# Adding the causal mask on VectorE, inside the search for the maximum, in the one-head banks of a differential-attention layer

## The chip, the cores and the metric

The kernel runs on one core of one Trainium2 chip. The metric is the device time of one execution in microseconds, as the median of three runs. One more execution was taken by the hardware profiler; every duration and share below is from that one.

## What is computed

Two layers run one after the other on an input of 4 sequences of 1024 tokens with 128 features. Each layer is x + s * silu(g), with s an attention and g a mixture of experts, both of the layer-normalized x.

Layer 0 is an attention of 16 heads with relative positions, without a causal mask. Layer 1 is a causal differential attention, and the change is there:

```python
q = (x @ Wq.T).reshape(B, S, 2 * H, hd).transpose(0, 2, 1, 3) * scaling   # 2H = 16 heads, hd = 8
k = (x @ Wk.T).reshape(B, S, 2 * H, hd).transpose(0, 2, 1, 3)
...
scores = jnp.einsum('bhqd,bhkd->bhqk', q, k)
causal = jnp.triu(jnp.full((S, S), -jnp.inf, dtype=scores.dtype), 1)
attn = jax.nn.softmax(scores + causal, axis=-1)
attn = attn.reshape(B, H, 2, S, S)
w = attn[:, :, 0] - lam * attn[:, :, 1]
```

A softmax needs the largest score of each row. The kernel finds it ahead of the exponentials, in what it calls a search.

## The kernel before

**Tiling.** Tokens go in tiles of 128, so a sequence has 8 tiles. Heads go in groups of 4 (HG). A step is one layer, one sequence, one group of heads and one pair t of query tiles, with m = 0 or 1 in the pair, so that the query tile is i = 2t + m. There are 64 steps in each layer. A step of layer 1 runs through key blocks 0 to 2t + 1, and each of them is one slot of the written-out order. In a slot TensorE forms the transposed scores of four heads (st, line 911), ScalarE takes their exponential (eT, line 949), and TensorE multiplies it with the values one slot later (o, line 958). The row maximum, negated and cut in three bfloat16 parts (lines 869, 884, 886), has been written as extra rows into the queries by then, so that the product of line 911 comes out with the maximum already taken off.

**Searches.** Some slots ahead of a step, TensorE forms the same scores untransposed into a PSUM bank of 512 columns (s, line 792, in score), and VectorE takes the maximum of each row (mx, line 852, in causal1). For a query tile i there are n = i + 1 key blocks, cut into a first part of up to 4 blocks and a second part of the rest. A part of one block puts four heads in one bank, a part of two blocks puts two, and parts of three or four blocks put one head in a bank. The part that ends at the diagonal has to be masked. TensorE does that by a product of the identity with a triangle of 0 and -3e38 (mask_q, bfloat16), which it accumulates onto the last 128 columns of each head (masked, line 831). The transposed scores are masked in the same manner with mask_k, also on line 831; there the bank is named st.

**The order.** Nothing is left to a scheduler. A list of slots is gone through one by one; every piece of work has been given its slot in advance, and within a slot the order in which the code calls is the order of each engine. Searches go two to a slot (RATE), and end 7 slots ahead of their step (LEAD). The expert products of layer 1 (lines 634 and 654), the next sequence's preparation and the routing (lines 534 to 566, VectorE) are spread over the slots. Engines meet by semaphores alone. The banks s, bank, turned_m and turned all come from one pool of three PSUM banks (ps_s), so TensorE can fill a bank only after VectorE has read what was in it three allocations earlier. At the end of a step VectorE copies the sums out of PSUM (os, line 969), and TensorE turns them (turned, line 977).

**A form that exists already.** Layer 0's near0 adds the position bias and takes the maximum in one call of tensor_tensor_reduce (line 808). In the trace that call is two instructions of VectorE: CUSTOM_DVE_ANT_0, which adds, writes the sum and keeps the maximum, and DVE_READ_ACCUMULATOR2_ANT, which writes the maximum out. Searches of that form alternate with plain ones there (far0, line 827).

**Pools.** The pool two has two buffers for each tag. The tag rows holds layer 0's position rows (line 722 fills them on ScalarE, line 731 completes them on GpSimd, a DMA stores them), and is not used in layer 1.

Of the kernel before, what the change touches and what calls it, by code (L numbers as in the profile page):

```python
# [9 lines left out]
F32 = mybir.dt.float32  # L10
# [3 lines left out]
ALU = mybir.AluOpType  # L14
AX = mybir.AxisListType

P = 128
NB = 4
# [4 lines left out]
HG = 4  # L23
NG = NH // HG
NQ = 4
# [4 lines left out]
FMAX = 3.4028234663852886e38  # L30

FLOOR = -3.4028232635611926e38
MASK = -3.0e38
GW = 512
BW = 3 * P
# [28 lines left out]
def both_layers(ctx, tc, a, out, x1d, g1d, flag):  # L64
    nc = tc.nc
    const = ctx.enter_context(tc.tile_pool(name="const", bufs=1))
    one = ctx.enter_context(tc.tile_pool(name="one", bufs=1))
    two = ctx.enter_context(tc.tile_pool(name="two", bufs=2))
# [62 lines left out]
    for pre in ("L0_attn_", "L1_attn_"):  # L131
# [28 lines left out]
        pattern=[[1, NE]],  # L160
        base=-NE,
        channel_multiplier=0,
# [126 lines left out]
    for m in range(2):  # L289
        pair = []  # L290
        for side in "lr":
            t = const.tile([NR, HG, S], BF16, tag=f"ks{side}{m}", name=f"ks{side}{m}")
# [4 lines left out]
    for m in range(2):  # L297
        t = const.tile([P, HG, GW], F32, tag=f"pos{m}", name=f"pos{m}")
# [3 lines left out]
    for m in range(3):  # L302
        t = dconst.tile([P, HG, GW], F32, tag=f"skew{m}", name=f"skew{m}")
# [7 lines left out]
    def after(n, f):  # L311

        if clock[0] is None or n == 0:
            f()
        else:
            todo.setdefault(clock[0] + n, []).append(f)
# [364 lines left out]
    def load_keys(q, g):  # L681
        q.ks[g] = turn("ks", stacks)
        n = 0
        for t, d in zip(q.ks[g], q.kd):
            view = d.rearrange("(h r) t -> r h t", r=3 * HD)[:, g * HG : (g + 1) * HG, :]
            for s in range(3):
                after(n, lambda t=t, s=s, v=view: nc.sync.dma_start(t[24 * s : 24 * s + 24], v))
                n += 1

    def load_queries(st):  # L690
        q, g, t = st.q, st.g, st.t
        st.qs = six.tile([NR, HG, 2 * P], BF16, tag="qs", name="qs")
        view = q.qd.rearrange("(h r) t -> r h t", r=QP * HD)

        def rows(s):
            nc.sync.dma_start(
                st.qs[24 * s : 24 * s + 24],
                view[8 * s : 8 * s + 24, g * HG : (g + 1) * HG, t * 2 * P : (t + 1) * 2 * P],
            )

        for s in range(3):
            after(s, lambda s=s: rows(s))
# [5 lines left out]
    def position_rows(st, m, k):  # L708

        if k == 0:  # L710
            st.pos[m] = two.tile([P, HG, BW], F32, tag="rows", name="rows")
        rows = st.pos[m]
        ps = bank()
        for j in range(2):
            nc.tensor.matmul(  # L715
                ps[:, j * 256 : (j + 1) * 256],
                lhsT=st.qs[:NS, 2 * k + j, m * P : (m + 1) * P],
                rhs=fs,
                start=True,
                stop=True,  # L720
            )
        nc.scalar.copy(  # L722
            rows[:, 2 * k : 2 * k + 2, 0:256], ps.rearrange("p (m v) -> p m v", v=256)
        )
        if k == 0:
            return
        skew = turn("skew", skews)
        st.pos[m] = (skew, rows)
        after(
            1,  # L730
            lambda: nc.gpsimd.tensor_copy(  # L731
                rows[:, :, 256:], rows[:, :, 255:256].to_broadcast([P, HG, P])
            ),
        )
        after(2, lambda: nc.sync.dma_start(skew[:, :, P:], rows))

    def position_keys(st, m):


        i = 2 * st.t + m  # L740
        skew, rows = st.pos[m]
        pos = turn("pos", pos_tiles)
        at, c0, n = (0, P, 2 * P) if i == 0 else (P, 0, 2 * P) if i == NT - 1 else (0, 0, BW)
        nc.sync.dma_start(
            pos[:, :, at : at + n],
            bass.AP(
                tensor=skew.tensor,
                offset=skew.offset + 127 + c0,
                ap=[[HG * GW - 1, P], [GW, HG], [1, n]],
            ),  # L750
        )
        if i == 0:
            nc.gpsimd.tensor_copy(
                pos[:, :, 2 * P : BW], rows[:, :, 255:256].to_broadcast([P, HG, P])
            )
        elif i == NT - 1:
            nc.gpsimd.memset(pos[:, :, 0:P], 0.0)
        st.pos[m] = pos
# [32 lines left out]
    def score(ps, st, m, j, keys, lo, hi, start=True, stop=True):  # L791
        nc.tensor.matmul(  # L792
            ps,
            lhsT=st.qs[:NS, j, m * P : (m + 1) * P],
            rhs=keys[:NS, j, lo * P : hi * P],
            start=start,
            stop=stop,
        )
# [30 lines left out]
    def masked(ps, mask, opens):  # L829

        nc.tensor.matmul(
            ps,
            lhsT=identb,
            rhs=mask.unsqueeze(1).to_broadcast([P, ps.shape[1], P]),
            start=opens,
            stop=not opens,
        )

    def causal1(st, m, heads, lo, wide, slot, n):
        (keys,) = st.q.ks[st.g][:1]  # L840
        diagonal = lo + wide == n
        w = wide * P
        ps = ps_s.tile([P, 512], F32, tag="s", name="s")
        parts = ps[:, : len(heads) * w].rearrange("p (j k) -> p j k", k=w)
        if wide == 1:
            masked(parts, mask_q, True)
        for k, j in enumerate(heads):
            last = wide == 1 and j == heads[-1]
            score(parts[:, k, :], st, m, j, keys, lo, lo + wide, wide > 1, last or not diagonal)
            if diagonal and wide > 1:  # L850
                masked(parts[:, k : k + 1, w - P :], mask_q, False)
        nc.vector.tensor_reduce(  # L852
            largest(st)[:, m, heads[0] : heads[-1] + 1, slot],
            parts,
            AX.X,
            ALU.max,
        )

    def largest(st):
        if st.mx is None:  # L860
            ns = 2 if st.q.layer == 0 or st.t >= 2 else 1
            st.mx = four.tile([P, 2, HG, ns], F32, tag="mx", name="mx")
        return st.mx

    def maxima(st, m):

        if m == 0:
            st.nm = four.tile([P, 2, HG], F32, tag="nm", name="nm")
        nc.vector.tensor_reduce(st.nm[:, m], largest(st)[:, m], AX.X, ALU.max, negate=True)  # L869

    def lower(st, m, j):

        i = 2 * st.t + m
        lo = (max(i - 1, 0) - first_key(i)) * P
        hi = (min(i + 2, NT) - first_key(i)) * P
        cols = st.sp[m][:, j * BW + lo : j * BW + hi]
        nc.scalar.activation(cols, cols, AF.Identity, bias=st.nm[:, m, j : j + 1])  # L877
# [197 lines left out]
    for q in seqs:  # L1075
        q.ks, q.hid = {}, {}
        q.first = len(slots)
        for g in range(NG):
            for t in range(NQ):
                st = Step(q, g, t)  # L1080
# [7 lines left out]
    def at(slot, f, where=None):  # L1088
        slot = math.floor(slot)
        if slot < 0:  # L1090
            early.append((slot, len(early), f))
        else:
            (todo if where is None else where).setdefault(slot, []).append(f)
# [5 lines left out]
    for n in reversed(range(len(steps))):  # L1099
        st = steps[n]  # L1100
# [6 lines left out]
    for n, jobs, times in reversed(job_slots):  # L1107
        st = steps[n]
        q = st.q
        first = times[0]  # L1110
        if st.t == 0:
            free = begin[n - NQ] + 1 if n >= 2 * NQ else -len(slots)
            at(max(first - 14, free), lambda st=st: load_keys(st.q, st.g))
        at(first - (10 if q.layer else 18), lambda st=st: load_queries(st))
        if q.layer == 0:
            for m in range(2):
                need = times[8 * m]
                for k in range(2):
                    s = math.floor(need) - 12 + 2 * k
                    at(s, lambda st=st, m=m, k=k: position_rows(st, m, k))  # L1120
                    taken.add(s)
                at(need - 4, lambda st=st, m=m: position_keys(st, m))
        for f, s in zip(jobs, times):
            at(s, f, searches)

        cut = 2 * HG if q.layer == 0 else st.searches
        for m, end in ((0, times[cut - 1]), (1, times[-1])):
            at(end + 1, lambda st=st, m=m: maxima(st, m))
            if q.layer == 0:
                for j in range(HG):  # L1130
                    at(end + 1 + j, lambda st=st, m=m, j=j: lower(st, m, j))
        at(times[-1] + 1, lambda st=st: split_maxima(st))
        s = math.floor(times[-1]) + 3
        at(s, lambda st=st: spread_maxima(st), urgent)
# [46 lines left out]
    first = prepare(seqs[0])  # L1181
# [25 lines left out]
    for k, q in enumerate(seqs):  # L1207
        if k + 1 < len(seqs):
            work = [f for f, _ in prepare(seqs[k + 1])]
            banked = [(f, True) for f in work]  # L1210
            turned, queries, keys, values = banked[2:4], work[4:7], work[7:10], banked[10:]
            queries = [(queries[0], True), (queries[1], True), (queries[2], False)]
            keys = [(keys[0], True), (keys[1], True), (keys[2], False)]
# [25 lines left out]
    with tc.manual_schedule():  # L1239
        last = None  # L1240
        s = 0
        while s < len(slots) or any(k >= s for k in todo) or last:
            clock[0] = s
            ready = None
            if s < len(slots):
                st, jb = slots[s]
# [5 lines left out]
            if last:  # L1252
                weigh(*last)
                st, jb = last[:2]
# [3 lines left out]
            last = ready  # L1258
# [5 lines left out]
    ps = bank()  # L1264
# [256 lines left out]
```

## Time and profile before

| | |
|---|---|
| median of three runs | 2108.15 us (2107.84 to 2114.01) |
| the profiled execution: its time | 2105.83 us |
| the profiled execution: its span, first to last instruction | 2104.1 us |
| layer 1's searches in that span | 1198 to 2060 us |
| TensorE's busy share of the span | 93% |
| VectorE's busy share of the span | 76% |
| mean granted TensorE clock | 0.965 |

The busy share of TensorE is not a measure of how close it is to its limit, since products overlap and their ends are modelled: a product of 128 columns lasts 220 ns in the record, and the next begins well before it has ended. What a product costs TensorE is read from the start of one to the start of the next, or from the pieces of the chain of waits, which counts it that way. The same holds for VectorE: the search of 512 columns lasts about 685 ns, and the next instruction can start about 600 ns after it did.

### The profile page before, as it was taken

How to read it: one execution, taken by the hardware profiler on the slowest of the kernel's cores; microseconds unless marked ns; L12 is line 12 of the kernel's file. 1: busy time of each engine (PE TensorE's matmuls, PEld its weight loads, DVE VectorE, ACT ScalarE, POOL GpSimd, SP SyncE). 2: the span in 40 equal slices, each digit the busy share in tenths (PEclk: the TensorE clock that was granted, in tenths of full speed). 3: DMA queues.
4: the chain of work that ended last, by engine and by line, in shares of the span. 5: the costliest groups of instructions: out<-in, count | busy, mean ns of one | idle time of the engine just before them, and what ended most of it. 6: DMA issues, size and time to landing. Idle time of an engine off the chain costs nothing.

```text
span 2104.1 us, 45540 instructions
## 1 busy us (share of the span) xinstructions
PE 1954.9 (93%) x17424; PEld 1110.8 (53%) x17424; DVE 1600.4 (76%) x4197; ACT 1329.2 (63%) x1801; POOL 586.0 (28%) x907
## 2 busy tenths in 40 slices
PE   3799999999999999999999989999999999999996
PEld 1355455555555555555455545565655555555553
DVE  4688788788888877887888887769776877687563
ACT  1577778777788777887778744554455445554543
POOL 3013332234322233322233213413241324122122
PEclk8699899999999999999999999999999999999997
DMA  4766666776777667767667421202120112111001
GB/s 124 253 200 207 202 215 205 218 223 216 224 221 217 218 185 230 224 198 230 190 209 216 133 84 34 64 22 57 34 64 22 49 40 64 23 25 54 23 5 33
DMA packets 232975, 286.98 MB, mean 136 GB/s; under 512 B 14932, under 2 KB 206972, under 8 KB 232492
## 3 DMA queue, kind: packets, MB, share of 16 engines
q1 hardware_dynamic: 228272, 282.38, 44.8%
q8 instruction: 139, 2.28, 0.5%
q10 hardware_dynamic: 4476, 1.60, 0.3%
q14 instruction: 88, 0.72, 0.1%
HBM read 153.28 MB, written 129.76 MB: 135 GB/s over the span
## 4 chain that ended last, share of the span: by engine, by line
PE 69%; DVE 17%; DMA 7%; POOL 2%; issue 2%; ACT 1%; SPq 1%; ACTq 0%; DVEq 0%; POOLq 0%
PE o L958 15%; PE s L792 15%; PE st L911 9%; PE st L943 7%; PE bank L654 6%; PE hid_ps L634 5%; DVE mx L852 4%; DMA qs<-qd 3%; DVE sp L808 2%; PE bank L599 2%; PE bank L715 2%; DVE m L884 2%; DMA pos<-skew 1%; DVE mrest L886 1%; PE bank L428 1%
## 5 line engine op out<-in xcount | busy, mean ns | idle before, releaser
L949 ACT ACTIVATE eT<-st 128x1024 f32<-128x1024 f32 x832 | 822.9, 991 | 512.2 <-PE st L911 466.2
L792 PE MATMUL s<-ksl,qs 72*128 72x384 bf16 (+3 forms) x1984 | 534.7, 313 | 21.9 <-DVE mx L827 7.7
L958 PE MATMUL o<-eT,va 128*9 128x256 f32 (+2 forms) x6656 | 522.0, 381 | 4.0 <-ACT eT L949 3.6
L827 DVE TENSOR_REDUCE mx<-s 128x1 f32<-128x512 f32 x512 | 352.8, 689 | 115.5 <-PE s L792 110.3
L852 DVE TENSOR_REDUCE mx<-s 128x1 f32<-128x512 f32 (+3 forms) x608 | 390.8, 656 | 34.8 <-PE s L792 17.4
L808 DVE CUSTOM_DVE_ANT_0 sp<-s,pos 128x512 f32<-128x512 f32 x512 | 352.5, 688 | 70.4 <-PE s L792 37.8
L792 PEld LDWEIGHTS <-qs 72*128 72x128 bf16 x2496 | 202.0, 98 | 381.7 <-issue 352.6
L877 ACT ACTIVATE sp<-sp,nm 128x384 f32<-128x384 f32 (+1 forms) x512 | 297.8, 583 | 102.9 <-DVE nm L869 102.7
L911 PE MATMUL st<-qs,ksl 75*128 75x256 bf16 (+1 forms) x2304 | 329.8, 253 | 0.0
L911 PEld LDWEIGHTS <-ksl 75*128 75x128 bf16 x2304 | 215.2, 99 | 68.9 <-issue 33.1
L943 PE MATMUL st<-ident,sp 128*128 128x128 f32 x1408 | 216.8, 280 | 0.0
L958 PEld LDWEIGHTS o<-eT,va 128*9 128x9 f32 (+1 forms) x6656 | 112.0, 91 | 187.5 <-issue 125.1
L731 POOL COPY rows<-rows 128x512 f32<-128x512 f32 x128 | 78.9, 617 | 430.8 <-ACT rows L722 381.8
L943 PEld LDWEIGHTS st<-ident,sp 128*128 128x128 f32 x1408 | 175.7, 145 | 25.8 <-issue 17.0
L669 POOL TENSOR_TENSOR g<-g,part 128x512 f32<-128x512 f32 x64 | 81.2, 1269 | 373.3 <-DVE part L662 309.5
L722 ACT COPY rows<-bank 128x512 f32<-128x512 f32 x256 | 147.6, 578 | 47.3 <-PE bank L715 37.8
L662 DVE TENSOR_TENSOR part<-bank,r1hot 128x512 f32<-128x512 f32 x64 | 44.3, 692 | 165.4 <-PE bank L654 152.5
L792 PE MATMUL s<-ksr,qs 72*128 72x128 bf16 (+3 forms) x512 | 157.8, 309 | 10.5 <-DVE mx L827 5.3
L715 PE MATMUL bank<-fs,qs 72*128 72x256 bf16 x512 | 101.1, 282 | 43.5 <-DMA qs<-qd 12.7
L654 PEld LDWEIGHTS bank<-pos,hid 128*128 128x128 f32 x1024 | 121.5, 192 | 21.8 <-DVE mx L852 11.1
L654 PE MATMUL bank<-pos,hid 128*128 128x128 f32 x1024 | 127.8, 278 | 5.3 <-DVE mx L852 4.8
L911 PE MATMUL st<-qs,ksr 75*128 75x256 bf16 (+1 forms) x768 | 124.2, 262 | 0.0
(209 smaller groups left out, 2174.0 us busy)
## 6 DMA issues: line engine op xcount, KB each, us to landing
skew<-rows SPq DMA_DIRECT2D x128, 768.0 KB
pos<-skew SPq DMA_DIRECT2D x96, 768.0 KB
qs<-qd SPq DMA_DIRECT2D x384, 48.0 KB
ksl<-kd SPq DMA_DIRECT2D x96, 192.0 KB
pos<-skew SPq DMA_DIRECT2D x32, 512.0 KB
kd<-piece SPq DMA_DIRECT2D x36, 256.0 KB
ksr<-kd SPq DMA_DIRECT2D x48, 192.0 KB
qd<-piece SPq DMA_DIRECT2D x35, 256.0 KB
```

The lines of the kernel that those rows point to most:

```text
L654: nc.tensor.matmul(ps[:, m * P : (m + 1) * P], lhsT=h[:, c, m * P : (m + 1) * P], rhs=w2t[:, 2 * e + c, :], start=(c == 0), stop=(c == 1),)
L715: nc.tensor.matmul(ps[:, j * 256 : (j + 1) * 256], lhsT=st.qs[:NS, 2 * k + j, m * P : (m + 1) * P], rhs=fs, start=True, stop=True,)
L722: nc.scalar.copy(rows[:, 2 * k : 2 * k + 2, 0:256], ps.rearrange("p (m v) -> p m v", v=256))
L792: nc.tensor.matmul(ps, lhsT=st.qs[:NS, j, m * P : (m + 1) * P], rhs=keys[:NS, j, lo * P : hi * P], start=start, stop=stop,)
L808: nc.vector.tensor_tensor_reduce(out=st.sp[m][:, j * BW : j * BW + 512], in0=ps, in1=st.pos[m][:, j, :], scale=1.0, scalar=-FMAX, op0=ALU.add,
L827: nc.vector.tensor_reduce(largest(st)[:, m, j, 1:2], ps, AX.X, ALU.max)
L852: nc.vector.tensor_reduce(largest(st)[:, m, heads[0] : heads[-1] + 1, slot], parts, AX.X, ALU.max,)
L877: nc.scalar.activation(cols, cols, AF.Identity, bias=st.nm[:, m, j : j + 1])
L911: nc.tensor.matmul(ps[:, j, lo * P : hi * P], lhsT=keys[side][:, j, jb * P : (jb + 1) * P], rhs=st.qs[:, j, lo * P : hi * P], start=start, ...
L943: nc.tensor.transpose(ps[:, j, m * P : (m + 1) * P], st.sp[m][:, at : at + P], ident)
L949: nc.scalar.activation(eT[:, :, skip:], ps[:, :, skip:], AF.Exp)
L958: nc.tensor.matmul(o_ps[32 * j : 32 * j + va.shape[-1], skip : 2 * P], lhsT=va, rhs=eT[:, j, skip:], start=(jb == st.blocks[0]), stop=(jb ...
```

## The change

In a bank with the diagonal and one head (query tiles 2, 3, 6 and 7 of a sequence, four heads, four groups, four sequences: 256 searches of layer 1), the mask product is no longer issued. VectorE's plain maximum is replaced there by the call that layer 0 uses: it reads the scores from PSUM and a mask from SBUF, adds them, writes the sums to a scratch tile that nothing reads, and keeps the maximum. Banks of two and four heads, and the transposed scores, are masked on TensorE as before.

The mask is a tile of 512 columns, zero but for the triangle in its last 128, of which the last w columns are used. It is made once by GpSimd (a memset and an affine_select), nine slots ahead of layer 1's first search. It and the scratch tile sums take the two buffers of the tag rows.

```diff
+    aside = {}
+
+    def wide_mask():
+        for name in ("mask", "sums"):
+            t = two.tile([P, HG, BW], F32, tag="rows", name=name)
+            aside[name] = t.rearrange("p j k -> p (j k)")[:, :512]
+        nc.gpsimd.memset(aside["mask"], 0.0)
+        last = aside["mask"][:, 3 * P :]
+        nc.gpsimd.affine_select(
+            out=last,
+            in_=last,
+            compare_op=ALU.is_ge,
+            fill=MASK,
+            base=0,
+            pattern=[[-1, P]],
+            channel_multiplier=1,
+        )
...
     def causal1(st, m, heads, lo, wide, slot, n):
...
         parts = ps[:, : len(heads) * w].rearrange("p (j k) -> p j k", k=w)
+        if diagonal and len(heads) == 1:
+            score(ps[:, :w], st, m, heads[0], keys, lo, lo + wide)
+            nc.vector.tensor_tensor_reduce(
+                out=aside["sums"][:, :w],
+                in0=ps[:, :w],
+                in1=aside["mask"][:, 512 - w :],
+                scale=1.0,
+                scalar=-FMAX,
+                op0=ALU.add,
+                op1=ALU.max,
+                accum_out=largest(st)[:, m, heads[0], slot : slot + 1],
+            )
+            return
         if wide == 1:
             masked(parts, mask_q, True)
...
+        if n == NB * NG * NQ:
+            at(first - 9, wide_mask)
```

## The prediction

> **What bounds the kernel now.** I read the stretch of layer 1's searches first, then the chain of waits in layer 1, then the groups of instructions that the change touches, last single slots in order of time. The first fence is the row of that stretch (columns: length, busy time and count of PE, PEld, DVE, ACT, POOL, then the granted clock, DMA share, GB/s), and the chain's summary from 1198 us to the end.
>
> ```profile
> 1198.00:2060.00 862.00, 826.20 (x7372) 491.54 (x7369) 637.49 (x1630) 434.25 (x506) 229.01 (x352) 0.99 0.15 41
> by line: PE bank L654 13.4%; PE o L958 13.1%; PE hid_ps L634 12.2%; PE s L792 11.8%; PE st L911 10.2%; DVE mx L852 9.3%; DVE m L884 2.3%; PE st L831 2.3%; PE s L831 2.1%; issue 1.7%; DVE os L969 1.4%; DVE mrest L886 1.2%; PE bank L428 1.0%;
> ```
>
> TensorE bounds layer 1, at full clock (0.99), so cutting products is worth something. But VectorE is busy for 74% of it, and the searches (DVE mx L852) hold 9.3% of the chain themselves: in some stretches it is VectorE that TensorE waits for. The mask products of the searches (PE s L831) hold 2.1% of 906 us, 19 us, and that includes the ones of banks with two and four heads, which stay.
>
> The groups by shape: mean ns is the second number after the bar.
>
> ```profile
> L852 DVE TENSOR_REDUCE mx<-s 128x1 f32<-128x512 f32 x384 | 259.7, 685 | 19.0 <-PE s L792 10.9 <-PE s L831 5.6
> L831 PE MATMUL s<-mask_q,identb 128*128 128x128 bf16 x384 | 81.6, 221 | 0.0
> L852 DVE TENSOR_REDUCE mx<-s 128x1 f32<-128x384 f32 x128 | 67.5, 546 | 2.1 <-PE s L831 1.4
> L808 DVE CUSTOM_DVE_ANT_0 sp<-s,pos 128x512 f32<-128x512 f32 x487 | 335.3, 688 | 67.0 <-PE s L792 36.0 <-ACT eT L949 19.0 <-PE bank L715 6.8
> L808 DVE DVE_READ_ACCUMULATOR2_ANT mx<- 128x1 f32 x486 | 40.4, 83 | 0.0
> ```
>
> Of the 384 mask products of 128 columns, 256 go. The two last rows are layer 0's use of the form that comes in: 688 ns against 685 for the same width, plus a second instruction of 83 ns. Then single slots, first TensorE and the chain's pieces there, then VectorE in layer 0, then a stretch where VectorE is the chain:
>
> ```profile
> 1607.82 0.33 PE L792 MATMUL s<-ksl,qs 72*128 72x384 bf16 x1
> 1607.98 0.22 PE L831 MATMUL s<-mask_q,identb 128*128 128x128 bf16 x1
> 1608.13 0.22 PE L892 MATMUL turned_m<-identb,m 128*12 128x128 bf16 x1
> ...
> 1607.98 0.16 PE s L792
> 1608.14 0.06 PE s L831
> ...
> 605.08 0.69 DVE L808 CUSTOM_DVE_ANT_0 sp<-s,pos 128x512 f32<-128x512 f32 x1
> 605.70 0.08 DVE L808 DVE_READ_ACCUMULATOR2_ANT mx<- 128x1 f32 x1
> ...
> 1658.67 0.17 DVE L886 TENSOR_TENSOR mrest<-mrest,m 128x8 f32<-128x8 f32 x1
> 1658.87 0.17 DVE L884 CAST m<-mrest 128x8 bf16<-128x8 f32 x1
> 1658.95 1.61 DVE L852 TENSOR_REDUCE mx<-s 128x1 f32<-128x512 f32 x3
> ...
> 1666.76 1.79 DVE mx L852 x3
> ```
>
> The chain charges the mask product 0.06 us, not 0.22: it overlaps with its neighbours.
>
> **Part 1, removed from TensorE.** From start to start a mask product takes 58 to 60 ns when the next product is of the same kind; before lines 958 and 892 it takes 149, but a score product shows the same extra there (311 for 512 columns against 226). So 58 ns each, and 256 x 0.058 = 14.8 us of TensorE. The 256 weight loads of identb go too; they lie under the score product (98 ns under 160 to 220), so I cost them at nothing: without them the next load lies under the same product. I matched the chain's pieces with the 256 products one by one: 168 are on it. First order: -168 x 0.058 = -9.8 us. The other 88 fall where VectorE holds TensorE up, or where TensorE has slack.
>
> **Part 2, VectorE's instruction itself.** A plain search lets the next instruction start 597 ns after it started (512 columns) or 464 (384). The custom one hands over after 605, and the instruction behind it then takes about 5 ns longer when a read stands between (602 against 597 for the same copy). So about 15 ns for each search, not 83: 256 x 0.015 = 3.8 us of VectorE. For 384 columns no row exists; the trace's step from 384 to 512 (133 ns) is kept, so 472 in place of 464. [...] The trace shows the read hidden in its neighbours, so I take 3.8 and keep 256 x 0.091 = 23 (read fully paid) as the upper end, and as the lower 256 x 0.008 = 2.0.
>
> **Part 3, a new wait on VectorE.** All 256 calls write the one scratch tile, so each but the first waits for the one before it; the built program has this wait ahead of 189 of them, and in the others an earlier wait covers it. Where something else ran between, it is long satisfied. Where two changed searches follow directly, and VectorE's order has 83 such pairs, the second is held until the read of the first has ended. In layer 0 the form alternates with plain searches, and none of its 254 such waits ever held, so no row prices this one. Nearest is a chain of waited instructions: the two rows at 1658.67 and 1658.87 show the second starting 33 ns after the end of the first, while the unwaited search after them starts 0.09 before its predecessor's end. Hence start to start 612 + 83 + 33, and some 20 for the extra wait instruction, about 750 against 597: 150 ns for a pair. Pairs that are further apart than that today pay nothing. 54 of the 83 are at 463 to 468 or 596 to 607 ns now, and the shortfall over all is 8.2 us. [...] The trace speaks for a price, so I take 8.2. The upper bound is 0.25 us a pair, 21 us for all 83. Queued behind a held search are the next searches, the copy os (L969, for which TensorE's turning on L977 waits) and the cut of the maximum (L884, L886), whose result goes to the queries; TensorE waits for the bank.
>
> **How much of parts 2 and 3 shows.** VectorE is given 12.0 us. Today 38 of the changed searches lie on the chain, 11 of them second in a tight pair: 38 x 0.015 + 11 x 0.15 = 2.2 us. The other 43 tight pairs (6.5 us) are covered by VectorE's idle time or by TensorE's lead of up to three banks. But several run in rows of three, up to a half microsecond late, just before the copy os, and TensorE now arrives earlier; I take 40% as coming through, 2.6 us (ends 0 and 6.5).
>
> **Part 4, once.** The mask: a memset of 512 columns, 0.52 us by the same shape on L757, and the select on 128 columns, on POOL. In its order they stand before the pos memset at 1178.92, ahead of which POOL idled 2.29 us; that covers them, and at most 0.8 us comes out if not. Its wait is for a store of rows whose data position_keys has to load anyway. SP's and ACT's orders do not change.
>
> **Sum**: -9.8 + 2.2 + 2.6 = -5.0 us on the profiled execution (2105.83, span 2104.1), to about 2100.8. The runs' median is 2.3 us above that execution, so 2108.15 - 5 = 2103. About 0.3%, 6.3 us, is what a measurement of this kernel can tell from no change, so this is a gain, but most likely below that.
>
> **Rivals.** [...]
> *B, VectorE becomes the bound.* The read holds the engine for its 83 ns and a held search waits 0.25 us: 23 + 21 = 44 us on VectorE, half of it exposed, 22 against 14.8 saved at most: +7, 2115. It decides from the point where more than 14.8 us of VectorE's addition is exposed (9.8 if TensorE saves only on the chain). For: tight pairs stand where VectorE is late already. Against: layer 0's rows, where the read costs 5 ns.
> *C, nothing arrives.* TensorE, earlier by 58 ns at a search, waits as much longer for banks, exponentials and copies: -2 to +2, 2106 to 2110.
>
> **Chances.** My forecast 0.55 (its own range 2099 to 2107; a third of it beyond the 6.3 us), A 0.17, B 0.13, C 0.15. Faster by over 0.3%: 0.55 x 0.33 + 0.17, about 0.35. Slower: B and a little of C, 0.15. Within: 0.50. The range takes A's far end and part of B: 2095 to 2112.
>
> **What would show it.** Right: line 831 on s falls from 416 to 160; the custom row in layer 1 means about 690 ns at 512 and 550 at 384 with a read of 83; in tight pairs starts lie about 750 (615) ns apart; the chain's PE s L831 falls to about 1%, DVE mx and os rise. [...]

## The result, and the profile after

The change makes the kernel slower. Over 20 executions of each, the median went from 2108.04 us (2096.48 to 2120.57) to 2115.12 us (2107.33 to 2134.20); the ratio is 1.0049, with a 95% interval of 1.0031 to 1.0067, so about 10 us. The forecast was 2103, with 2095 to 2112 as the range.

The profiled execution of the changed kernel has a span of 2111.3 us, against 2104.1. First the row of the searches' stretch (length, busy time and count of PE, PEld, DVE, ACT, POOL, then granted clock, DMA share, GB/s) and the chain of waits in layer 1. Below line 836 line numbers are 33 higher after than before: the plain search is L885, the copy of the sums L1002, its turning L1010, the transposed scores L944. L867 is the new call.

```profile
1198.00:2060.00 862.00, 808.92 (x7019) 474.81 (x7018) 636.29 (x1867) 430.51 (x500) 227.79 (x349) 0.98 0.15 41
by line: PE bank L654 13.0%; PE hid_ps L634 12.0%; PE o L991 11.3%; PE s L792 9.4%; PE st L944 8.1%; DVE mx L885 7.5%; issue 4.2%; DVE sums L867 4.2%; DVE m L917 3.0%; PE st L831 1.8%; DVE mrest L919 1.8%; DVE os L1002 1.6%; DMA qs<-qd 1.6%
```

TensorE has 353 products fewer in the same 862 us; 256 of them are the ones that went, and most of the others come after 2060 us now, since the kernel is later. Its searches' products and outputs have lost share of the chain (PE s L792 11.8% to 9.4%, PE o 13.1% to 11.3%). VectorE's searches have gained it: L885 and L867 together 11.7%, where L852 alone had 9.3%. The calls' 4.2% are 39 us; matched piece by piece, the chain of before spent 25 us on the same 256 searches. "issue", time with no cause in the record, went from 1.7% to 4.2%. The clock went from 0.99 to 0.98.

The groups of the new call by shape (busy us, mean ns after the bar):

```profile
L867 DVE CUSTOM_DVE_ANT_0 sums<-s,mask 128x512 f32<-128x512 f32 x128 | 87.8, 686 | 9.6 <-PE s L792 2.9
L867 DVE CUSTOM_DVE_ANT_0 sums<-s,mask 128x384 f32<-128x384 f32 x128 | 70.2, 549 | 6.2 <-PE s L792 0.8 <-PE turned_m L925 0.4 <-PE st L944 0.2
L867 DVE DVE_READ_ACCUMULATOR2_ANT mx<- 128x1 f32 x256 | 20.7, 81 | 0.0
```

The call costs what layer 0's row said: 686 ns and 549 beside 685 and 546 of the plain search. But there are 9.6 and 6.2 us of idle time in front of the calls, and only 2.9 and 1.4 have a named cause. VectorE in order of time shows what they are. This is the place of the three searches in one row at 1666.76 us before:

```profile
1673.23 0.68 DVE L867 CUSTOM_DVE_ANT_0 sums<-s,mask 128x512 f32<-128x512 f32 x1
1673.84 0.08 DVE L867 DVE_READ_ACCUMULATOR2_ANT mx<- 128x1 f32 x1
1674.07 0.69 DVE L867 CUSTOM_DVE_ANT_0 sums<-s,mask 128x512 f32<-128x512 f32 x1
1674.68 0.08 DVE L867 DVE_READ_ACCUMULATOR2_ANT mx<- 128x1 f32 x1
1674.91 0.69 DVE L867 CUSTOM_DVE_ANT_0 sums<-s,mask 128x512 f32<-128x512 f32 x1
1675.53 0.08 DVE L867 DVE_READ_ACCUMULATOR2_ANT mx<- 128x1 f32 x1
1675.53 0.67 DVE L577 COPY wT<-bank 8x512 f32<-8x512 f32 x1
```

The copy starts with the read ahead of it, at 1675.53: the read is nearly free, as was said. The second and third call start 0.84 us after the one before, not 0.60: each is held until the first read has ended, and then for 144 ns more. That is the median over all 83 directly following pairs, at both widths. Start to start the median is 844 ns (512 columns) and 700 (384), where plain searches in direct succession took 597 and 464; the expectations below have 838 and 699 for it. The prediction had 750 and 615.

TensorE feels it behind the copy of the sums and at the banks. The longest waits of TensorE's weight loads for VectorE from 1243 to 2060 us (total us, times, longest), before and then after:

```profile
PEld bank L654 <- DVE mx L852: 11.1, 20, 1.3
PEld turned L977 <- DVE os L969: 10.5, 35, 0.8
```

```profile
PEld turned L1010 <- DVE os L1002: 15.6, 37, 0.8
PEld bank L654 <- DVE mx L867: 8.0, 16, 0.8
PEld bank L654 <- DVE mx L885: 6.1, 8, 1.3
```

**A measure for the clock.** The granted clock was left out of the prediction's sum, and it matters. In the records of before and after TensorE's granted clock is 1.0 or 0.5 in each of the 30 stretches that either has, and nothing between. An execution's half-clock time is taken here as twice its span times what its mean granted clock lacks to 1. Over 148 executions of the kernel before, on three chips, its time rises by 0.44 us for each us of it (correlation 0.92; 0.41 to 0.46 on each chip alone, and 0.49 in 23 executions on a fourth), and it explains most of the scatter of 10 us to either side. So beside the plain difference I give one with the half-clock time taken out at 0.43 us for each us, which is much sharper. This is a correlation, and it counts the whole execution: in the profile before, 102 of the 149 us at half clock lie ahead of 1198 us, in a part that the change does not touch.

### The profile page after: what moved, and what is told of

Its sections match the earlier page's. It is cut to its first block, busy times and chain, and to the rows that moved or that the text cites. A ratio compares the mean times of both kernels' runs of the same rounds, so it can differ in the third digit from the quotient of the medians.

```text
span 2111.3 us, 45474 instructions
## 1 busy us (share of the span) xinstructions
PE 1948.5 (92%) x17168; PEld 1100.5 (52%) x17168; DVE 1606.5 (76%) x4453; ACT 1330.6 (63%) x1801; POOL 587.8 (28%) x909
## 4 chain that ended last, share of the span: by engine, by line
PE 65%; DVE 19%; DMA 7%; issue 3%; POOL 2%; ACT 2%; SPq 1%; ACTq 0%; DVEq 0%; POOLq 0%
PE o L991 15%; PE s L792 14%; PE st L944 8%; PE st L976 7%; PE bank L654 6%; PE hid_ps L634 5%; DMA qs<-qd 4%; DVE mx L885 3%; DVE m L917 2%; DVE sp L808 2%; PE bank L599 2%; PE bank L715 2%; DVE sums L867 2%; DVE mrest L919 1%; PE bank L428 1%
## 5 line engine op out<-in xcount | busy, mean ns | idle before, releaser
L792 PE MATMUL s<-ksl,qs 72*128 72x384 bf16 (+3 forms) x1984 | 535.5, 313 | 25.6 <-DVE mx L827 7.7
L792 PEld LDWEIGHTS <-qs 72*128 72x128 bf16 x2496 | 202.1, 98 | 386.2 <-issue 350.7
L944 PE MATMUL st<-qs,ksl 75*128 75x256 bf16 (+1 forms) x2304 | 329.2, 253 | 0.0
L885 DVE TENSOR_REDUCE mx<-s 128x1 f32<-128x512 f32 (+2 forms) x352 | 239.0, 685 | 29.0 <-PE s L792 19.9
L944 PEld LDWEIGHTS <-ksl 75*128 75x128 bf16 x2304 | 217.1, 99 | 71.1 <-issue 31.8
L867 DVE CUSTOM_DVE_ANT_0 sums<-s,mask 128x384 f32<-128x384 f32 (+1 forms) x256 | 158.1, 617 | 15.8 <-PE s L792 3.6
L792 PE MATMUL s<-ksr,qs 72*128 72x128 bf16 (+3 forms) x512 | 157.9, 310 | 11.7 <-DMA ksr<-kd 6.3
```

Of the source, the lines that this page charges most:

```text
L792: nc.tensor.matmul(ps, lhsT=st.qs[:NS, j, m * P : (m + 1) * P], rhs=keys[:NS, j, lo * P : hi * P], start=start, stop=stop,)
L867: nc.vector.tensor_tensor_reduce(out=aside["sums"][:, :w], in0=ps[:, :w], in1=aside["mask"][:, 512 - w :], scale=1.0, scalar=-FMAX, op0=AL ...
L885: nc.vector.tensor_reduce(largest(st)[:, m, heads[0] : heads[-1] + 1, slot], parts, AX.X, ALU.max,)
L944: nc.tensor.matmul(ps[:, j, lo * P : hi * P], lhsT=keys[side][:, j, jb * P : (jb + 1) * P], rhs=st.qs[:, j, lo * P : hi * P], start=start, ...
```

## The experiments

Theories, as the expectations number them. 1: the held pairs, priced too low, ate the gain, and half-clock time added to it (1b: the clock falls because TensorE has less to do; 1c: because VectorE makes it wait). 2: the call with its read is dear by itself. 3: the change costs nothing, and a late transfer at the start of layer 1 and a low clock came by chance.

Means of the differences to the kernel before on the same chip, with 95% intervals; ratios are of the executions too. In the last column the half-clock time is taken out.

| kernel | executions | ratio (95%) | time, us | half-clock time, us | clock taken out, us |
|---|---|---|---|---|---|
| e4 changed again | 22 | 1.0044 (1.0029-1.0059) | +8.3 ± 2.4 | +12.6 ± 5.9 | +2.8 ± 1.3 |
| e2 product removed, plain maximum | 22 | 0.9982 (0.9967-0.9996) | -3.0 ± 2.4 | +8.3 ± 5.2 | -6.6 ± 1.1 |
| e3 call, product kept | 13 | 1.0063 (1.0040-1.0086) | +14.6 ± 3.7 | +13.6 ± 6.8 | +8.7 ± 1.4 |
| e5 call without hold, product kept | 14 | 0.9989 (0.9965-1.0013) | -2.3 ± 4.2 | -4.9 ± 8.6 | -0.2 ± 1.5 |
| e1, e8 changed, without hold | 25 | 0.9976 (0.9948-1.0005), 0.9975 (0.9950-1.0001) | -4.4 ± 3.4 | +4.5 ± 7.1 | -6.3 ± 1.0 |
| e6 heads 0 and 2 alone | 22 | 0.9979 (0.9959-0.9998) | -4.9 ± 3.3 | +0.1 ± 6.6 | -5.0 ± 1.2 |
| e7, e9 without hold, sequences 1 to 3 | 40 | 0.9970 (0.9952-0.9988), 0.9959 (0.9938-0.9981) | -8.5 ± 2.2 | -8.1 ± 4.8 | -5.0 ± 0.8 |
| e10 product removed, sequences 1 to 3 | 17 | 0.9953 (0.9934-0.9972) | -6.7 ± 3.7 | -1.6 ± 8.3 | -6.0 ± 1.2 |
| e12 changed, sequences 1 to 3 | 12 | 1.0042 (1.0013-1.0071) | +8.2 ± 5.6 | +13.3 ± 10.8 | +2.5 ± 2.0 |
| e11 kernel before again | 12 | 0.9988 (0.9961-1.0015) | +0.8 ± 5.1 | +0.4 ± 10.9 | +0.6 ± 1.5 |

### e1 and e8: the change without the hold

```diff
-            aside[name] = t.rearrange("p j k -> p (j k)")[:, :512]
+            flat = t.rearrange("p j k -> p (j k)")
+            aside[name] = flat[:, :512]
+        aside["parts"] = [flat[:, 512 * k : 512 * k + 512] for k in range(3)]
...
-                out=aside["sums"][:, :w],
+                out=turn("sums", aside["parts"])[:, :w],
```

> The changed kernel, but the call writes its sums in turn to three parts of the scratch tile, so that no search waits for the one before it (VectorE's 189 waits on itself go; nothing else changes). Theory 1 (the held pairs, priced too low, and the half-clock windows that longer VectorE stretches bring, ate the gain): directly following custom searches start about 615 ns apart at 512 columns and 480 at 384 instead of 838 and 699; with 13 us less on VectorE the span falls below the kernel before, by 3 to 9 us, and layer 1's half-clock time comes back from 27 us toward 17. Theory 2 (the call itself, with its read, makes VectorE late whatever the waits): it stays within 3 us of the changed kernel. Theory 3 (layer 1 started on a late transfer and the clock fell by chance, the change has no cost): this and the repeated changed kernel are alike.

> The three scratch parts again, since their first interval reached from 11 us faster to 1 us slower. Expected 3 to 7 us faster than before, granted clock 0.961 to 0.963; with the half-clock time taken out, 6 us below before and 8 below the changed kernel.

The function `turn`, which the kernel has already, hands out the three parts one after another. The same three calls in e8, where the call stands on line 869:

```profile
1668.32 0.68 DVE L869 CUSTOM_DVE_ANT_0 sums<-s,mask 128x512 f32<-128x512 f32 x1
1668.92 0.08 DVE L869 DVE_READ_ACCUMULATOR2_ANT mx<- 128x1 f32 x1
1668.92 0.69 DVE L869 CUSTOM_DVE_ANT_0 sums<-s,mask 128x512 f32<-128x512 f32 x1
1669.53 0.08 DVE L869 DVE_READ_ACCUMULATOR2_ANT mx<- 128x1 f32 x1
1669.54 0.69 DVE L869 CUSTOM_DVE_ANT_0 sums<-s,mask 128x512 f32<-128x512 f32 x1
1670.16 0.08 DVE L869 DVE_READ_ACCUMULATOR2_ANT mx<- 128x1 f32 x1
```

0.60 to 0.62 us apart: the hold is gone with the shared scratch tile, read and call remain. Over e1 and e8 the time is 4.4 us below before, and with half-clock time taken out 6.3 below it and 9.1 below the changed kernel. Theory 1's first half, the held pairs, holds, and theory 3 falls. Its second half stays open here: half-clock time was to come back, and at +4.5 ± 7.1 it lies between before and changed. Each of the two intervals of the ratio still touches 1.

### e2: the product alone

```diff
-            nc.vector.tensor_tensor_reduce(
-                out=aside["sums"][:, :w],
-                in0=ps[:, :w],
-                in1=aside["mask"][:, 512 - w :],
...
+            nc.vector.tensor_reduce(
+                largest(st)[:, m, heads[0], slot : slot + 1], ps[:, :w], AX.X, ALU.max
+            )
```

> The product alone is taken away: in the 256 banks TensorE issues no mask product and VectorE takes the plain maximum as before, so those searches take the maximum over the masked scores too (the mask is left out of them). It gives what 256 x 58 ns of TensorE is worth with VectorE unchanged. All theories of the loss say a gain; by the chain's count 9.8 us, up to 13 with what falls off the chain, less 2 us for new waits on banks: 2095 to 2100. Should it bring less than 4 us, the removed product was never worth its 58 ns (rival C), and part 1 of the sum is wrong.

Only 3.0 us, and 6.6 with half-clock time taken out: less than any theory allowed. To see where the rest went I set the start of each TensorE product against that of the same product before, from 1243 to 2060 us, without the stretches in which either runs at half clock. The steps toward earlier sum to 11.6 us; steps of over 25 ns toward later give 5.7 back, at waits for VectorE: the copy os, the banks, the rows of the maximum. Net -5.9, in line with the -6.6. TensorE is earlier by 58 ns at a product, and at the next place where VectorE sets the time it waits that much longer. That is rival C, for half of the gain.

### e3 and e5: the call alone, with and without the hold

```diff
-            score(ps[:, :w], st, m, heads[0], keys, lo, lo + wide)
+            score(ps[:, :w], st, m, heads[0], keys, lo, lo + wide, True, False)
+            masked(parts[:, 0:1, w - P :], mask_q, False)
```

The affine_select is dropped in both, so the mask tile is zero; e5 has the three parts of e1 as well.

> The call alone: TensorE's mask products stay in the 256 banks, and VectorE makes the call with a tile of zeros in place of the mask. It gives what the call with its wait costs with TensorE unchanged. Theory 1: 83 pairs held, 13 us more on VectorE, half to all of it shown, and more half-clock time: 10 to 20 us slower than before, and the difference to the changed kernel is what e2 gains. Theory 3: no more than 3 us slower than before.

> The call with three scratch parts (no search held), and TensorE's mask products kept in the 256 banks; the mask tile is zero. TensorE's work is that of the kernel before, VectorE has the call and its read but no wait on itself. Clock by activity (theory 1b: the clock falls because TensorE has less to do in windows that are already thin): granted clock as before, 0.9630 to 0.9645, time within 4 us of before. Clock by VectorE (theory 1c: the clock falls because VectorE's call makes TensorE wait): clock 0.960 to 0.962 with the products kept, and 4 us or more slower than before.

e5 settles theory 2: 256 calls with their reads cost -0.2 ± 1.5 us. e3 differs from it by the hold, and stands at +8.7 ± 1.4. The same comparison of starts finds steps toward later of 1.5 us in e5 and of about 7.5 in e3, and at most 2 us toward earlier; the largest group in e3 is the turning behind the copy os, some 3 us.

The clock moves with the hold too. Both keep TensorE's products and make VectorE's calls, and their half-clock times, +13.6 ± 6.8 and -4.9 ± 8.6, do not overlap; they ran on different chips, each beside the kernel before. So the hold lowers the clock (1c); for 1b these two say nothing. In the changed kernel the two can't be told apart: e4, with holds, has +12.6, and e2, without a hold, +8.3, and the difference between them on their one chip is 4.3 ± 6.6.

### e4 and e11: the changed kernel and the kernel before, again

> The changed kernel again on this chip, as the measure for the other three. Theory 1: 5 to 12 us slower than before, mean granted clock lower by 0.002 to 0.004, layer 1's half-clock time above 20 us. Theory 3: its half-clock time is as in the kernel before (17 us), and it is within 4 us of it.

> The kernel before against itself, to see what such a comparison makes of no difference, in time and in clock: within 3 us, half-clock time within 7 us, and within 1.5 us with half-clock time taken out. If it is further off than that, the clock differences told of the other runs are not to be trusted.

Both came as expected. e11 shows what these comparisons make of no difference: below 1 us in each column, with intervals that are among the widest of the table.

### e6: every other head

```diff
-        if diagonal and len(heads) == 1:
+        if diagonal and len(heads) == 1 and heads[0] % 2 == 0:
```

> The change for heads 0 and 2 of a group alone, with the one scratch tile; heads 1 and 3 keep mask product and plain maximum. 128 products go, and no two calls follow each other directly, so hardly one is held. If the holds are the loss (theory 1): half of TensorE's gain at equal clock, 3 us less than before, granted clock between that of before and of the changed kernel, time 0 to 4 us below before. If the call costs by itself (theory 2): half of the changed kernel's loss, 3 to 5 us slower than before.

With one scratch tile but no two calls in a row, half of the products bring -5.0 ± 1.2 with the clock taken out, against -6.3 ± 1.0 and -6.6 ± 1.1 for all of them, and half-clock time is that of before. More than the half that was expected came, though the intervals are too wide to say how much more; that the products that stay lie where VectorE sets the time would fit, and was not tested.

### e7, e9, e10 and e12: sequences 1 to 3 alone

Each adds `and st.q.b > 0` to the condition: in e7 and e9 to e1, in e10 to e2, in e12 to the changed kernel.

> Three scratch parts, but the change only in sequences 1 to 3 of layer 1; the first one, whose start holds most half-clock time in the profiles (1230 to 1275 us), keeps the products. If the clock is lost by the products that are missing at that start: clock 0.0005 to 0.001 above that of all four sequences with three parts, and the time 1 us or more below it in spite of a quarter of the products. If it is lost everywhere alike: a quarter of the gain of three parts is lost, about 1.5 us slower than it.

> Three scratch parts in sequences 1 to 3 alone, again: the fastest so far, 8 us below before with a granted clock 0.0016 above it. If keeping the products at the start of layer 1 keeps the clock up, the clock is again at or above that of before and the time 5 to 9 us below it. If the high clock was chance, half-clock time is 4 to 8 us above before and the time 2 to 4 us below; with half-clock time taken out it is 5 us below before either way.

> The product alone is taken away, in sequences 1 to 3 alone (192 of the 256 searches; those take the maximum over the masked scores too). With half-clock time taken out: three quarters of the 6.6 us of all four sequences, 5 us below before. If the clock is lost at the first sequence's start, half-clock time is as in before, against 8 us more with all four; if it is lost wherever products go, it is 6 us above before.

> The changed kernel with its one scratch tile, held pairs and all, in sequences 1 to 3 alone. With half-clock time taken out: three quarters of the changed kernel's loss, 2 us above before. If the first sequence's start is where the clock is lost, half-clock time is as in before and the time 0 to 3 us above it; if the holds lose it wherever they are, half-clock time is 8 us or more above before and the time 5 us or more above it.

e7 and e9 are the fastest version that was run, and beat both kernels: medians 2102.53 and 2102.69, with 2110.99 and 2113.05 for the kernel before beside them. With the clock taken out they bring 5.0 us, as three quarters of the products should. The rest is clock: 8.1 us less half-clock time than before. Their two profiles do not show it where the change is: from 1198 us on they have 54 and 62 us at half clock, against 47 and 56 in the two profiles of before, and ahead of it, where nothing was changed, 79 and 82 against 102 and 113. That speaks for chance, but two profiles can't settle it for 40 executions. I had thought that the clock was lost where products are missing at the start of layer 1. e12 speaks against it for the holds: the first sequence is untouched there, and half-clock time is up by 13.3 all the same, with an interval that reaches from 2 to 24. For products that are missing without a hold the runs do not decide: +8.3 and +4.5 in four sequences, -1.6 and -8.1 in three.

## Why the prediction was wrong

**Part 3, the hold: a term of the sum with the wrong size.** The wait was seen, and the pairs that it hits. The step that failed is its price: it was taken from instructions that wait inline (33 ns after the end) and 20 ns for the extra wait instruction, because no row was thought to price it. It is 144 ns after the end of the read. The pairs fall short by 13.6 us in all (844 or 700 ns less the spacing of before, 63 pairs), not 8.2.

The trace of before had the price. That layer 0's calls always alternate with plain searches, and that none of their waits ever held, is not so: at 65 and at 71 us two of them follow directly.

```profile
65.07 0.68 DVE L808 CUSTOM_DVE_ANT_0 sp<-s,pos 128x512 f32<-128x512 f32 x1
65.67 0.08 DVE L808 DVE_READ_ACCUMULATOR2_ANT mx<- 128x1 f32 x1
65.90 0.69 DVE L808 CUSTOM_DVE_ANT_0 sp<-s,pos 128x512 f32<-128x512 f32 x1
66.52 0.08 DVE L808 DVE_READ_ACCUMULATOR2_ANT mx<- 128x1 f32 x1
```

Start to start that is 0.83 us, and the second call starts 144 ns after the end of the read, at both places, as in the held pairs of layer 1. From this row part 3 would have come out near its right size.

The wait has its price in the pair as a whole: 611 ns from call to call without it in e8, 844 with it (medians). Part of the 144 ns is the separate wait instruction. In the trace of before L995 always follows L993 and waits for it, 45 times within the instruction itself and 19 times by a separate wait instruction in front (the second place below):

```profile
1232.14 0.23 DVE L993 TENSOR_SCALAR rinv<-rinv,lam 128x4 f32<-128x4 f32 x1
1232.41 0.29 DVE L995 TENSOR_TENSOR both<-turned,rinv 128x128 f32<-128x128 f32 x1
1258.39 0.23 DVE L993 TENSOR_SCALAR rinv<-rinv,lam 128x4 f32<-128x4 f32 x1
1258.72 0.29 DVE L995 TENSOR_TENSOR both<-turned,rinv 128x128 f32<-128x128 f32 x1
```

From end to start it takes 34 or 35 ns in the first form and 104 or 105 in the second (one of the 19 took longer). So the separate wait costs about 70 ns there; where the other 40 ns of the 144 come from is open.

**How much shows.** I let 11 tight pairs on the chain and 40% of the rest through, 4.8 of 12.0 us. The hold alone is worth 9.1 ± 1.6 us (+2.8 for e4 less -6.3 for e1 and e8, clock taken out), about two thirds of 13.6; e3 less e5 gives 8.9. By the comparison of starts the changed kernel gains 12.3 us and gives 14.4 back, e8 gains 12.1 and gives 5.6 back; of the 14.4, 4 to 5 are at the turning behind os. So the pairs lie in stretches where VectorE is late already, and right before the copy os, and the idle time that was to cover them is elsewhere.

**Part 1, -9.8 us from the chain.** A product is worth its 58 ns where it is on the chain, but the chain does not say what is next. It brought 6.6 ± 1.1 (e2). The argument that 9.3% of the chain is "these very searches" counted all 608: 25 of those 84 us lay on the 256 that change.

**Part 2 was right.** 605 to 617 ns and 471 to 484 from call to read, the read free, nothing in e5. So was part 4 on GpSimd: behind the mask's memset and affine_select it still idled 1.45 us before the pos memset, where it had idled 2.29.

**What was not in the sum: the clock.** The prediction read the clock as full (0.99) and put its change at nothing, without a reason. The kernels with holds (e3, e4, e12: 47 executions) have 13.0 ± 4.4 us more half-clock time than before, 5.6 us of time. How a half-clock stretch comes about the profiles show only in part. Before and after, the stretch in which the second sequence's outputs wait for VectorE (columns as in the first fence, the clock third from the end):

```profile
1473.00:1477.00 4.00, 3.25 (x22) 2.25 (x23) 3.93 (x9) 1.02 (x1) 0.46 (x2) 0.60 0.00 0
1477.00:1481.00 4.00, 4.00 (x37) 2.42 (x30) 3.26 (x7) 1.03 (x1) 0.00 (x0) 0.97 0.09 28
```

```profile
1472.00:1478.00 6.00, 4.57 (x40) 2.56 (x41) 5.62 (x19) 2.05 (x2) 0.00 (x0) 1.00 0.22 81
1478.00:1482.00 4.00, 2.94 (x29) 1.84 (x26) 3.78 (x6) 1.02 (x1) 0.46 (x2) 0.99 0.00 0
1482.00:1488.50 6.50, 6.50 (x36) 3.45 (x35) 4.48 (x8) 1.82 (x2) 2.83 (x2) 0.50 0.07 19
```

Before, TensorE idles once for 1.05 us and then runs at half clock for 3.4 us. After, it idles twice for 1.05 us, with VectorE busy nearly throughout, and the half clock lasts 6.8 us, in which TensorE is busy all the time. But one sequence later, where TensorE idles twice for 1.05 us in both kernels, it is the other way round, 6.8 us before and 3.4 after:

```profile
1687.00:1692.30 5.30, 3.19 (x31) 2.18 (x31) 5.20 (x12) 1.02 (x1) 0.46 (x2) 1.00 0.01 3
1692.30:1699.10 6.80, 6.80 (x36) 3.96 (x38) 4.27 (x9) 1.44 (x2) 2.45 (x2) 0.50 0.05 15
```

```profile
1694.00:1700.30 6.30, 4.19 (x36) 2.77 (x37) 5.80 (x15) 1.02 (x1) 0.47 (x2) 1.00 0.01 3
1700.30:1703.80 3.50, 3.50 (x20) 1.95 (x18) 3.10 (x6) 1.02 (x1) 1.62 (x1) 0.51 0.11 30
```

So the number of idle stretches does not give the length. But for the last one, at the program's end, the half-clock stretches in these two records last 3.41 us or a multiple of it (6.83, 10.24, 13.65, and 54.61 at the start). What decides how long a half-clock stretch gets was not shown. Single profiles can't give the cause, and the 13 us rest on the executions.

**The sum mended.** With the clock taken out, e4 is +2.8 ± 1.3: -6.3 for the products with what they give back, and +9.1 for the hold. That is the same number taken apart and no test of it; a test is e2 and e3, each measured alone, -6.6 + 8.7 = +2.1. The clock adds 5.4 (12.6 us at 0.43), which makes the +8.3 measured. So the forecast of -5.0 missed by some 13 us: 3.5 that part 1 credited too much, 4.3 that parts 2 and 3 charged too little, and 5.4 of clock.

**The rivals.** A, whose far end was the range's 2095, fell: no run shows a gain of 13 us, the most that any brought was 8.5 (e7 and e9), and the changed kernel's waits were not free, with 844 ns from call to call in the held pairs where 597 stood before. C was right for half of part 1. B had the sign and the hold (0.25 us a pair), but not the read, and its condition was not met: it asked for more than 14.8 us to come through, and 9.1 came. The smaller gain and the clock did the rest.

**Left open.** Why e7 and e9 have less half-clock time than before; whether removed products alone cost clock, and so how much of the changed kernel's 12.6 us is the hold's; and a wait at the start of layer 1, told at the end.

## What to carry to other kernels

A scratch output that nothing reads still made each call here wait for the last one that wrote it (844 ns from call to call, 611 with three parts): give it as many parts as instructions can follow each other directly, before counting the rest of the change. Before pricing a new wait by analogy, search the whole trace for the same two instructions in direct succession; two places in another layer had the price here. Then weigh the wait by where its pairs lie, not by the engine's mean idle time: here they stood where the engine was already late, and 9.1 of 13.6 us came through. When work is taken off the bounding engine, look for the next place where another engine sets the time, and for the clock, which fell here when held calls made the bounding engine wait (+13.6 us at half clock in e3, -4.9 in e5).

## What was not expected of the hardware

A VectorE call that waits by a separate instruction for the one just before it starts 144 ns after that has ended; an instruction that waits inline starts 33 to 35 ns after (L884 behind L886, over 250 times in the trace of before), and a call without a wait about 82 ns before (e8). Time at half clock goes with 0.41 to 0.49 us of time for each us in this kernel, and a change that only moves VectorE (e3) came with 13.6 us more of it. At the start of layer 1 TensorE's wait for the first keys and queries was 4.0 to 4.5 us in the five profiles of kernels with all products or half of them, and 5.6 to 7.5 in the nine others, also in those that leave the first sequence as it was. The four whose kernels have no affine_select for the mask are all among the five, so products are not the only thing that sets the groups apart; the cause was not found, and these 2 to 3 us are in no sum above.
